# A fused adaLN transformer block on one core: the last group of block 0, the place of one k projection, and two waits of the MLP

## The chip, the cores and the metric

The kernel runs on one core of a Trainium2 chip. The metric is the device time of one execution in microseconds (us); the median of three timed runs of the kernel before is 3613.98 us (3611.85 to 3615.18). Engines are named as in the profile: PE is the matrix engine (PEld its weight loads), DVE the vector engine, ACT the scalar engine, POOL the GpSimd engine, SP the engine whose queue issues nearly all transfers.

## The reference

For eight sequences of 1024 tokens with 512 channels the reference computes one transformer block whose two normalizations are shifted and scaled by a condition:

```python
mod = silu(condition) @ Wada + bada
sh_a, sc_a, gt_a, sh_m, sc_m, gt_m = split(mod, 6, axis=1)
xm = layernorm(x, g1, be1) * (1 + sc_a) + sh_a
x = x + gt_a * attention(xm, Wqkv, Wproj, bproj)     # causal, 16 heads of 32 channels
xm = layernorm(x, g2, be2) * (1 + sc_m) + sh_m
x = x + gt_m * (gelu(xm @ W1 + b1) @ W2 + b2)        # W1: 512 x 2048, W2: 2048 x 512
```

All data are float32. In the softmax of a row, the exponentials are divided by their sum over all visible keys.

## The kernel before

**Blocks and groups.** The tokens are cut into 16 blocks of 512 (`blocks`): block n is half h = n % 2 of sequence n // 2. A block of half 0 sees 512 keys, a block of half 1 sees 1024. The 16 heads of a block are handled in four groups g of four heads. A group is cut into units of 512 columns; the triangular diagonal parts are packed, and the third triangle of an even group shares a unit with that of the odd group after it.

**Attention of one group.** `scores` makes q k^T into the one four-bank PSUM tile `st`, DVE adds the mask (L1403) and takes row maxima (L1406). `split_maxima` writes the maxima as three bf16 parts (L1425 to L1428), `maxima_rows` turns them into rows (L1444). `weights_T` then computes transposed scores minus the maxima into the same tile `st` (L1469, L1481), ACT takes the exponential into one of three SBUF slots `pT` (L1493), POOL zeroes the masked triangle (L1498). `weigh` multiplies by v into `po` (L1521). The sums of the exponentials are collected by `add_weights`: POOL adds every further unit's exponentials onto those of the group's first unit, head by head (L1594). `finish` then multiplies that one accumulated tile with a matrix of ones (L1539), which sums over the key partitions; ACT copies sums and numerators to `rec` and `top` (L1545, L1548; one buffer each), DVE inverts the sums in four reciprocals (L1554) and POOL multiplies (L1571) into the tile that held q. When `add_weights` is done with a unit, its slot goes back to `free_p`.

**The reciprocals are jobs.** `finish` does not issue the four reciprocals and the product itself; it puts them on the list `jobs`, which `run_jobs` empties one by one when, by the planner's reckoning, DVE is not behind PE.

**Linear work.** All projections (q, k, v, the MLP's up and down products) use a Strassen-like scheme of seven products instead of eight (`strassen`, `down`), all through three PSUM banks and the matmul at L201. A k, q or v projection is 7 products of 32 matmul records. Weight pieces of 256 KB come through a ring of nine buffers, filled in the order of use by `fetch` on SP whenever a piece is released. The sums of weight quarters that the scheme needs are made once: for q, k, v at the start, for W1 and W2 by the generator `preparation` (on DVE or POOL, `either`, L158 and L161), which also writes them to DRAM through SP (L687). A piece that is such a sum can be fetched only after that.

**Order of the work.** `plan[w]` lists the linear steps of window w, which is laid beside the attention of block w. Window 0 ends with `("k", 2)` and `("gates", "m")`; window 1 begins with the load of the residual of block 0, the gate rows, `("proj", 0)`, `("mt", 0)` (transposes of the normalized residual), `("q", 2)` and the up products of block 0. The steps run as one stream (`main`); parts that may run late (`tail`, `modulated`) are side threads. A step yields what it must wait for; `proj` of block n waits for `("attended", n)`, which is set when the last group's product has been issued.

**Interleaving.** The program is put in order when it is built, by a planner with costs in ns per instruction (`note`, `due`). Before each attention step, `step_aside` lets linear steps go first until they have done as much as is due by then, and further while the attention's inputs are not ready by that reckoning. What is due grows by each attention unit's need times `stream["rate"]`, which is the planned time of the window's steps over the block's need (times 0.7 in block 0). `scores` takes another way, `scores_by_heads` (L1357, L1376), when no linear step can run for the next 3000 ns: it uses the free banks for four single heads.

**Gate of the MLP.** The first up product of block 0, `("u", 0, 0)`, waits for `"prepared"`, which is set when `preparation` has made the sums of both matrices. `attend` drives all of it; the last unit of block 0's group 3 is closed (`close`, `finish`) after one more score unit, and then the remaining score units of block 1's group 0 and some of group 1 are issued.

Of the kernel before, what the change touches and what calls it, by code (L numbers as in the profile page):

```python
# [22 lines left out]
def kernel(  # L23
# [203 lines left out]
    def mlp_steps(n):  # L227
# [4 lines left out]
        + [("load_xa", 1), ("sums", "q", 0), ("k", 0), ("norm_a", 1), ("q", 0)]  # L232
        + [("sums", "v", 0), ("at", 1), ("v", 0)],
        0: [("load_xa", 2), ("preps",), ("k", 1), ("norm_a", 2), ("gates", "a"), ("q", 1)]
        + [("mod", 3), ("at", 2), ("v", 1), ("mod", 4), ("columns_m",), ("k", 2), ("gates", "m")],
    }
    late = []
    for w in range(1, NB):
        n = w - 1
        m = mlp_steps(n)  # L240
        even = blocks[n][1] == 0
        rows_a = [("rows", blocks[n][0], "a")] if even else []
        rows_m = [("rows", blocks[n][0], "m")] if even else []
        own = m[:1] + ([("load_xa", w + 2)] if w + 2 < NB else []) + m[1:3]
        own += [("norm_a", w + 2)] if w + 2 < NB else []
        if w == NB - 1:
            steps = late[:1] + [("load_xr", n)] + rows_a + [("proj", n), ("mt", n)] + late[1:]
            steps += [("v", w)] + rows_m + own + m[3:6]
            late = m[6:]
        else:  # L250

            steps = late + [("v", w), ("load_xr", n)] + rows_a + [("proj", n), ("k", w + 1)]
            if w == 1:
                steps = [("load_xr", n)] + rows_a + [("proj", n)]
            steps += [("mt", n), ("q", w + 1)] + rows_m + own
            at = [("at", w + 2)] if w + 2 < NB else []
            if blocks[w][1] == 0:

                steps += m[3:5]
                late = m[5:6] + at + m[6:]  # L260
            else:
                steps += m[3:6] + at
                late = m[6:]
        plan[w] = steps
# [440 lines left out]
    def preparation():  # L705


        todo = [(w, i) for w in (W1, W2) for i in range(NQ)]
        loaded = []

        def load(w, i):
            stage = act.tile([P, NC, TB], F32, tag="hT", name=f"prep_{LABEL[id(w)]}_{i}", bufs=NQ)
            got = {}
            for j, kf in enumerate(RAW):
                a = next(a for a in ("A11", "A12", "A21", "A22") if FULL[a] == kf)
                got[a] = stage[:, j, :]
                nc.sync.dma_start(got[a].rearrange("p (k n) -> p k n", n=HB), quarter(w, i, *kf))
            loaded.append((w, i, got, now["PE"] + 12000))

        load(*todo.pop(0))  # L720
        while loaded:
            if todo:
                load(*todo.pop(0))
            w, i, got, ready = loaded.pop(0)
            for out, a, b, op, name in IN_PLACE:
                yield ready
                keys = [("prep", w is W2, i, a), ("prep", w is W2, i, b)]
                either(got[out], got[a], got[b], op, keys, [("prep", w is W2, i, out)])
                keep(w, i, name, got[out])
# [209 lines left out]
    def up(step):  # L939
        _, n, q = step  # L940

        def gelu():
            for i in range(NC):
                f = q * NC + i
                nc.scalar.activation(  # L945
                    hT[:, i, :], hT[:, i, :], AF.Gelu, bias=cols[:, O_B1 + f : O_B1 + f + 1]
                )
                k = q // 2 + 1
                note_act(590, "gelu", [("h", n, q)], [(n, f"B{k}1"), (n, f"B{k}2"), ("g", n, q)])

        def finished():
            if q == NQ - 1:
                written["m used", n] = 0.0
            excursion(gelu, [("h", n, q)], first=True)

        if (n, q) == (0, 0):
            yield ["prepared"], []
        written["g", n, q] = NEVER
        hT = act.tile([P, NC, TB], F32, tag="hT", name=f"hT_{n}_{q}", bufs=NQ)
        hTs[n, q] = hT  # L960

        yield from strassen(
            step,
            f"m{n}",
            lambda f, t: hT[:, half(f, 2), half(t, HB)],
            ("h", n, q),
            False,
            finished,
        )
# [18 lines left out]
    def down(n, part):  # L988
# [79 lines left out]

        got = partials
        if part == 0:  # L1070
            yield [("g", n, 0), ("g", n, 1)], []
            for i in range(NTT):
                add_to(residual[n][:, i, :], gate_rows["gbm"], [("row", "gbm")], [("xr", n, i)])
            combine(nc.vector, "B12", "B12", "B11")
# [47 lines left out]
    def perform(step):  # L1122
# [28 lines left out]
        elif kind == "at":  # L1151
            n = step[1]
            guards = [("m used", n - 3)] if n > 2 else [("v done", 0)] if n == 2 else []
            start(modulated(f"a{n}", *columns_of["a"], blocks[n][0], guards))
        elif kind == "beside":
            start(perform(step[1]))
        elif kind == "sums":
            sum_weights(step[1:])
        elif kind == "mt":
            n = step[1]  # L1160
            guards = [("v done", n + 1)]
            start(modulated(f"m{n}", *columns_of["m"], blocks[n][0], guards))
        elif kind == "k":
            yield [("free for k", step[1])], []
            yield from project_T(step, kTs, kvp, "kT", lambda: None)
        elif kind == "q":
            yield from project_T(step, qTs, act, "qT", lambda: projected.add(step[1]))
        elif kind == "v":
            yield from project_v(step)
        elif kind == "preps":  # L1170
            prepared[0] = [preparation(), 0.0]
            written["prepared"] = NEVER
        elif kind == "rows":
            gate_broadcasts(*step[1:])
        elif kind == "proj":
            yield from project_out(step[1])
        elif kind == "u":
            yield from up(step)
        elif kind == "d":
            yield from down(*step[1:])  # L1180
# [272 lines left out]
            m_rows[n, g] = row  # L1453

    free_p = list(range(3))
    outs, totals = {}, {}

    def weights_T(n, g, parts):
# [72 lines left out]
    def finish(n, g):  # L1531

        run_jobs(True)
        acc, slot = totals.pop((n, g))
        step_aside([("acc", n, g)], [BANK])
        bank = lin_bank()
        for j in range(HPG):
            r = slice(j * hd, (j + 1) * hd)
            nc.tensor.matmul(banks[bank][r, :], ones[:, :hd], acc[:, j, :], start=True, stop=True)  # L1539
        note_pe(2 * COLUMN * TB, "columns", [("acc", n, g), ("p", slot)], [("l", bank)])  # L1540
        free_p.append(slot)
        top = tmp.tile([P, TB], F32, tag="top", name=f"top_{n}_{g}", bufs=1)
        rec = tmp.tile([P, TB], F32, tag="rec", name=f"rec_{n}_{g}", bufs=1)
        kr = "rec"
# [12 lines left out]
        if (n, g) == groups[-1]:  # L1557
# [4 lines left out]
                note("DVE", 200, [kr, "top"], [("att", n, i)])  # L1562
            return

        def quotient():
            invert(3)
            if n == NB - 1 and g == NC - 2:
# [13 lines left out]

    def add_weights(n, g, parts, pT, slot):

        acc, first = totals[n, g]
        for _, c0, w, _ in parts:
            for j in range(HPG):
# [65 lines left out]
    def close(n, g, parts, pT, slot, last):  # L1652
# [3 lines left out]
        weigh(n, g, own, pT, slot, last)  # L1656
        if other:
            shared[n, g + 1] = other, pT, slot
        elif parts[0][0] > 0:
            free_p.append(slot)  # L1660
        if parts[0][0] == 0:
            totals[n, g] = (pT, slot)
            if (n, g) in shared:
                more, pT, slot = shared.pop((n, g))
                weigh(n, g, more, pT, slot, False)
                add_weights(n, g, more, pT, slot)
                free_p.append(slot)
        if last:
            finish(n, g)

# [97 lines left out]
```

## Time and profile before

| what | value |
|---|---|
| median of three timed runs | 3613.98 us |
| the profiled execution: first to last instruction | 3610.1 us |
| PE busy | 3537.6 us, 98% |
| DVE, ACT, POOL busy | 58%, 37%, 56% |
| mean granted PE clock | 0.995 |
| transfers on SP's queue | 422.56 MB, 38.8% of the 16 DMA engines |

The page gives no time of the profiled execution other than its span; the timed runs are 1.7 to 5.1 us above it, which holds what lies around the first and the last instruction. In the timeline a row is a run of equal instructions: start, length, engine, line, operation, output <- inputs, shapes, count, and in brackets the idle time before it with what ended it. A float32 matmul of the program appears as two records, and four matmuls of 32 columns each run beside one another, so "x8" is one matmul for each of the four heads or column groups. A window row gives the busy time of each engine in a stretch, then the granted PE clock, the busy share of the DMA engines and their rate.

### The profile page before, as it was taken

What the parts mean: (1) busy time and instruction counts of PE and PEld (TensorE: products, weight loads), DVE (VectorE), ACT (ScalarE), POOL (GpSimd) and SP (SyncE); (2) the same over time, 40 slices, a digit from 0 to 9 for tenths busy, and PEclk for the clock granted to TensorE, in tenths of its full rate; (3) what the DMA queues carried; (4) which work ended last, traced back from release to release, by engine and by line L of the source; (5) the groups of instructions that cost most, each with busy time, mean ns of one, the idle gap of its engine ahead of it and who ended that gap; (6) DMA issues with size and microseconds to landing.
All of it is one profiled execution on the core that took longest, in us unless ns stands there. A gap on an engine that the chain in (4) does not pass through costs nothing.

```text
span 3610.1 us, 121129 instructions
## 1 busy us (share of the span) xinstructions
PE 3537.6 (98%) x54821; PEld 1777.0 (49%) x54821; DVE 2078.8 (58%) x2316; ACT 1325.9 (37%) x1388; POOL 2038.3 (56%) x2187
## 2 busy tenths in 40 slices
PE   8999999999999999999999999999999999999999
PEld 5434445445554455544555455454554545545445
DVE  6765675563755547465464655746557455564663
ACT  2335334252433523335243351424524244232421
POOL 3666746665456753666536665456654566544660
PEclk9989999999999999999999999999999999999999
DMA  6633333434343343433434334343343433435334
GB/s 202 220 117 104 109 104 110 127 98 128 112 118 110 104 133 113 133 92 98 133 109 148 91 93 132 105 141 101 99 128 105 139 101 101 124 92 155 90 111 138
DMA packets 307894, 430.35 MB, mean 119 GB/s; under 512 B 25900, under 2 KB 176236, under 8 KB 307380
## 3 DMA queue, kind: packets, MB, share of 16 engines
q1 hardware_dynamic: 307264, 422.56, 38.8%
q8 instruction: 432, 7.08, 0.8%
q14 instruction: 82, 0.67, 0.1%
q10 hardware_dynamic: 116, 0.03, 0.0%
HBM read 394.12 MB, written 28.38 MB: 117 GB/s over the span
## 4 chain that ended last, share of the span: by engine, by line
PE 90%; DVE 4%; POOL 2%; ACT 2%; issue 1%; DMA 0%; SPq 0%; ACTq 0%; DVEq 0%; POOLq 0%
PE bank L201 62%; PE st L1469 8%; PE sc L1389 8%; PE po L1521 7%; DVE mx L1406 2%; PE st L1481 2%; PE bank L641 2%; PE bank L1539 2%; POOL pT L1594 1%; POOL xr L161 1%; ACT pT L1493 1%; DVE hT L1003 0%; PE bank L1444 0%; DVE xr L158 0%; ACT hT L945 0%
## 5 line engine op out<-in xcount | busy, mean ns | idle before, releaser
L1594 POOL TENSOR_TENSOR pT<-pT,pT 128x384 f32<-128x384 f32 (+2 forms) x1266 | 1195.6, 981 | 400.4 <-PE po L1521 211.0
L1493 ACT ACTIVATE pT<-st 128x2048 f32<-128x2048 f32 x288 | 541.0, 1878 | 858.2 <-PE st L1481 826.5
L201 PE MATMUL bank<-w,hT 128*32 128x256 f32 x14336 | 805.6, 381 | 1.0 <-ACT rec L1545 0.9
L1406 DVE TENSOR_REDUCE mx<-sc 128x4 f32<-128x2048 f32 (+3 forms) x380 | 658.5, 1754 | 147.7 <-PE sc L1389 140.6
L201 PEld LDWEIGHTS bank<-w,hT 128*32 128x32 f32 x14336 | 455.2, 110 | 338.4 <-issue 42.7
L201 PE MATMUL bank<-xm_m,w 128*32 128x256 f32 x8192 | 498.3, 381 | 3.1 <-ACT xm_m L651 3.0
L201 PE MATMUL bank<-t_m,w 128*32 128x256 f32 x6144 | 392.2, 381 | 0.4 <-DVE t_m L660 0.4
L1498 POOL TENSOR_SCALAR_AFFINE_SELECT pT<-pT 128x512 f32<-128x512 f32 x256 | 162.1, 651 | 400.4 <-ACT pT L1493 400.4
L201 PEld LDWEIGHTS bank<-xm_m,w 128*32 128x32 f32 x8192 | 254.9, 110 | 229.9 <-issue 62.5
L1389 PE MATMUL sc<-kT,qT 32*128 32x512 f32 (+3 forms) x3040 | 331.6, 524 | 7.6 <-DVE mx L1406 7.0
L1469 PE MATMUL st<-qT,kT 32*128 32x512 f32 (+3 forms) x3072 | 330.9, 523 | 6.7 <-DVE mx L1406 5.0
L1403 DVE TENSOR_TENSOR sc<-sc,mask 128x1024 f32<-128x1024 f32 (+1 forms) x159 | 161.5, 1016 | 278.9 <-PE sc L1389 238.9
L1521 PE MATMUL po<-pT,v 128*32 128x512 f32 (+3 forms) x3072 | 305.8, 493 | 10.2 <-POOL pT L1498 10.2
L201 PEld LDWEIGHTS bank<-t_m,w 128*32 128x32 f32 x6144 | 187.1, 110 | 197.2 <-issue 81.7
L201 PE MATMUL bank<-xm_a,w 128*32 128x256 f32 x3968 | 239.8, 380 | 0.0
L201 PE MATMUL bank<-w,qT 128*32 128x512 f32 x2048 | 237.8, 595 | 0.0
L1554 DVE RECIPROCAL rec<-rec 128x128 f32<-128x128 f32 x256 | 226.0, 919 | 6.0 <-ACT rec L1545 6.0
L1389 PEld LDWEIGHTS sc<-kT,qT 32*128 32x128 f32 x3040 | 130.8, 184 | 175.7 <-ACT pT L1493 81.3
L1469 PEld LDWEIGHTS st<-qT,kT 32*128 32x128 f32 x3072 | 130.1, 184 | 164.4 <-issue 71.6
L1493 ACT ACT_TABLE_LOAD x88 | 112.9, 1283 | 205.8 <-PE st L1481 205.3
L201 PE MATMUL bank<-t_a,w 128*32 128x256 f32 x2944 | 188.5, 380 | 0.0
L193 DVE TENSOR_TENSOR hT<-bank,u_u 128x512 f32<-128x512 f32 x192 | 128.4, 683 | 97.0 <-PE bank L201 96.2
(207 smaller groups left out, 3521.3 us busy)
## 6 DMA issues: line engine op xcount, KB each, us to landing
w<-in_L_cond_W_dram SPq DMA_DIRECT2D x384, 256.0 KB
w<-kept_up_S SPq DMA_DIRECT2D x256, 256.0 KB
w<-kept_down_S SPq DMA_DIRECT2D x256, 256.0 KB
w<-kept_qkv_S SPq DMA_DIRECT2D x180, 256.0 KB
w<-in_L_cond_Wqkv_dram SPq DMA_DIRECT2D x147, 256.0 KB
hat<-in_x_dram SPq DMA_DIRECT2D x64, 256.0 KB
w<-in_L_cond_Wproj_dram SPq DMA_DIRECT2D x64, 256.0 KB
xr<-in_x_dram SPq DMA_DIRECT2D x64, 256.0 KB
```

What stands on the lines that cost most here:

```text
L193: nc.vector.tensor_tensor(out, src, other, op)
L201: nc.tensor.matmul(ps[r, :], lhsT[:, r], rhs, start=start, stop=stop, skip_group_check=True)
L641: nc.tensor.transpose(banks[bank][:, ts(t, P)], got[t][:, ts(c, P)], ident)
L1389: nc.tensor.matmul(sc[:, j, c0 : c0 + w], qTs[n][r, gg, ts(qt, P)], keys_of(n, kh)[r, gg, :w], start=True, stop=True, skip_group_check=True,)
L1403: nc.vector.tensor_tensor(place, place, shape_of.to_broadcast(place.shape), ALU.add)
L1406: nc.vector.tensor_reduce(maxima[n, gg][:, kh, qt, :], sc[:, :, c0 : c0 + w], axis=AX.X, op=ALU.max)
L1469: nc.tensor.matmul(st[:, j, c0 : c0 + w], kT[r, gg, ts(k % NTT, P)], qT[r, gg, TB - w :], start=(c0 == 0), stop=False, skip_group_check=True,)
L1493: nc.scalar.activation(pT[:, :, :used], st[:, :, :used], AF.Exp, scale=scale)
L1498: nc.gpsimd.affine_select(diagonal, diagonal, pattern=[[0, HPG], [1, P]], compare_op=ALU.is_ge, fill=0.0, base=0, channel_multiplier=-1,)
L1521: nc.tensor.matmul(po[r, TB - w :], v[:, k % NTT, g * P + j * hd : g * P + (j + 1) * hd], pT[:, j, c0 : c0 + w], start=(k == 0), stop=last ...
L1554: nc.vector.reciprocal(some, some)
L1594: nc.gpsimd.tensor_tensor(into, into, pT[:, j, c0 : c0 + w], ALU.add)
```

## The change

The plan moves `("k", 2)` from the end of window 0 to window 1, between the gate rows and `("proj", 0)`; `("gates", "m")` therefore follows `("columns_m",)` directly. In block 0's group 3 (`first_end`), `add_weights` no longer adds on POOL but keeps the units in `unadded`; their slots are held until `finish`, which sums all terms by ones matmuls into one bank, and then issues the four reciprocals and the product at once, the product on DVE. The wait for the weight sums is split: `"prepared up"` is set when the sums of W1 are done and is what the first up product waits for; every block's first down part now also waits for `"prepared"`.

```diff
         0: [("load_xa", 2), ("preps",), ("k", 1), ("norm_a", 2), ("gates", "a"), ("q", 1)]
-        + [("mod", 3), ("at", 2), ("v", 1), ("mod", 4), ("columns_m",), ("k", 2), ("gates", "m")],
+        + [("mod", 3), ("at", 2), ("v", 1), ("mod", 4), ("columns_m",), ("gates", "m")],
...
             if w == 1:
-                steps = [("load_xr", n)] + rows_a + [("proj", n)]
+                steps = [("load_xr", n)] + rows_a + [("k", w + 1), ("proj", n)]
...
             w, i, got, ready = loaded.pop(0)
+            if (w is W2, i) == (True, 0):
+                written["prepared up"] = 0.0
...
         if (n, q) == (0, 0):
-            yield ["prepared"], []
+            yield ["prepared up"], []
...
         if part == 0:
-            yield [("g", n, 0), ("g", n, 1)], []
+            yield [("g", n, 0), ("g", n, 1), "prepared"], []
...
-            written["prepared"] = NEVER
+            written["prepared up"] = written["prepared"] = NEVER
...
+    first_end, unadded = (0, NC - 1), []
...
-        step_aside([("acc", n, g)], [BANK])
+        more = unadded if (n, g) == first_end else []
+        step_aside([("acc", n, g), *(("p", slot) for *_, slot in more)], [BANK])
         bank = lin_bank()
-        for j in range(HPG):
-            r = slice(j * hd, (j + 1) * hd)
-            nc.tensor.matmul(banks[bank][r, :], ones[:, :hd], acc[:, j, :], start=True, stop=True)
-        note_pe(2 * COLUMN * TB, "columns", [("acc", n, g), ("p", slot)], [("l", bank)])
-        free_p.append(slot)
+        terms = [(0, TB, acc, slot)] + [(c0, w, pT, slot) for parts, pT, slot in more for _, c0, w, _ in parts]
+        for i, (c0, w, term, held) in enumerate(terms):
+            for j in range(HPG):
+                r = slice(j * hd, (j + 1) * hd)
+                nc.tensor.matmul(
+                    banks[bank][r, TB - w :], ones[:, :hd], term[:, j, c0 : c0 + w],
+                    start=i == 0, stop=i == len(terms) - 1, skip_group_check=True,
+                )
+            note_pe(2 * COLUMN * w, "columns", [("acc", n, g), ("p", held)], [("l", bank)])
+        free_p.extend([slot, *(held for *_, held in more)])
...
+        if (n, g) == first_end:
+            for i in range(NTT):
+                invert(i)
+            nc.vector.tensor_tensor(qTs[n][:, g, :], top, rec, ALU.mult)
+            note("DVE", 700, [kr, "top"], [("att", n)], port=True)
+            written["attended", n] = 0.0
+            return
...
     def add_weights(n, g, parts, pT, slot):
 
+        if (n, g) == first_end:
+            unadded.append((parts, pT, slot))
+            return
...
-        elif parts[0][0] > 0:
+        elif parts[0][0] > 0 and (n, g) != first_end:
             free_p.append(slot)
...
-                free_p.append(slot)
+                if (n, g) != first_end:
+                    free_p.append(slot)
```

## The prediction

> **What bounds the kernel now.** I read the page first, then the list of what PE waited for, then windows around the longest of these waits, then each engine's timeline there.
>
> ```profile
> span 3610.1 us, 121129 instructions
> PE 3537.6 (98%) x54821; PEld 1777.0 (49%) x54821; DVE 2078.8 (58%) x2316; ACT 1325.9 (37%) x1388; POOL 2038.3 (56%) x2187
> ```
>
> PE is the bound nearly everywhere, so a change can only win where PE stands or is slow. The waits list names one group above all, the scores by heads that wait for DVE. The windows show the place and a second price, the granted clock (PEclk):
>
> ```profile
> core 0: us, PE busy (x) PEld busy (x) DVE busy (x) ACT busy (x) POOL busy (x), PEclk, DMA share, GB/s
> 166.40:174.00 7.60, 7.57 (x56) 3.08 (x51) 5.85 (x6) 1.07 (x2) 5.62 (x6) 1.00 0.89 277
> 174.00:178.60 4.60, 0.14 (x4) 0.14 (x8) 4.53 (x7) 0.00 (x0) 4.37 (x4) 1.00 1.05 391
> 178.60:185.50 6.90, 4.48 (x26) 2.58 (x26) 6.76 (x13) 0.00 (x0) 0.23 (x1) 0.75 0.75 241
> 185.50:199.20 13.70, 10.46 (x50) 3.55 (x54) 12.47 (x15) 1.02 (x2) 6.92 (x9) 0.50 0.79 285
> 248.20:250.40 2.20, 0.16 (x5) 0.09 (x1) 1.74 (x3) 2.19 (x6) 0.00 (x0) 0.99 0.00 0
> 250.40:257.20 6.80, 6.55 (x32) 3.82 (x32) 3.74 (x3) 4.78 (x7) 0.00 (x0) 0.50 0.00 0
> ```
>
> PE work lost = length minus busy time times clock. 174.0 to 178.6: 4.60 - 0.14 = 4.5; to 185.5: 6.90 - 4.48 x 0.75 = 3.5; to 199.2: 13.70 - 10.46 x 0.50 = 8.5. Together **16.5 us**. The last two rows, another stall, lose 2.0 + 3.5 = 5.5. What PE lacked in the first stall:
>
> ```profile
> 157.30 9.23 POOL L1594 TENSOR_TENSOR pT<-pT,pT 128x256 f32<-128x256 f32 x12
> 195.80 1.26 POOL L1571 TENSOR_TENSOR qT<-top,rec 128x512 f32<-128x512 f32 x1 [3.61 <-DVE rec L1554]
> ```
> ```profile
> 173.43 0.93 DVE L1554 RECIPROCAL rec<-rec 128x128 f32<-128x128 f32 x1
> 181.71 0.94 DVE L1554 RECIPROCAL rec<-rec 128x128 f32<-128x128 f32 x1
> 187.96 0.94 DVE L1554 RECIPROCAL rec<-rec 128x128 f32<-128x128 f32 x1
> 194.72 0.94 DVE L1554 RECIPROCAL rec<-rec 128x128 f32<-128x128 f32 x1
> ```
> ```profile
> 178.46 0.81 PE L1357 MATMUL bank<-kT,qT 32*128 32x384 f32 x1 [4.49 <-DVE mx L1376]
> 198.66 3.01 PE L201 MATMUL bank<-w,qT 128*32 128x512 f32 x24
> ```
>
> The ones matmul of block 0's group 3 waits for twelve POOL additions (to 166.5). Its four reciprocals then lie on DVE one by one between score reductions, over 21 us, and only then POOL makes the product. Projection 0 (w,qT) starts at 198.66. In front of it the linear stream is empty, and score units, which DVE takes 2.3 to 3.6 us each for, are all PE has.
>
> **The change part by part.**
>
> *Sums on PE.* Twelve POOL additions (9.23 us) go. In their place come ones matmuls of 384, 128 and 256 columns. In `po` rows of this shape 384 + 128 take 0.86 us in the chain and 256 take 0.46, so **+1.3 us** on PE. The last `po` of the group ends at 159.2, so the sums can end at 159.2 + 0.86 + 1.3 = 161.4 instead of 168. Three `pT` slots stay held until then, which is no later than before (166.8), so the next exponentials wait for nothing new.
>
> *Weighed against the skill.* The Trainium skill, "Perfetto Trace Analysis", Identifying the Most-Contended Engine, says to improve the engine with the highest occupancy first. Read so, this part is wrong way round: PE has 98%, POOL 56%, and the sum would be +1.3 us and nothing gained. The window rows of 174 to 199 decide for me: there PE is not the contended engine.
>
> *Reciprocals at once.* `rec` and `top` have one buffer, so ACT's copy waits for group 2's product. That stood behind the additions (166.49); without them it follows group 2's last reciprocal (161.8) and ends at 163.1. Then: copy 0.58, four reciprocals 4 x 0.92 = 3.7, product. The product moves from POOL (1.28) to DVE; its one row there is 1.64 us, other DVE products of two SBUF tiles of this size 0.68 to 1.7, so 0.7 to 1.7. A score reduction of 2.29 may lie in front. The result stands at 163.1 + 0.6 + 3.7 + 0.7 to 1.7 + 0 to 2.3 = 168.1 to 171.4, against 197.1. Queued behind these 4.4 to 5.4 us on DVE are one reduction and one bank's copy; PE has three banks and other work, so I cost that wait at nothing, and at up to 2.3 us if the banks are all full.
>
> *k 2 as cover.* 7 x 32 records at 1.72 us per 32: 12.0 us, moved, not added. Gates m (16 records, 3.6 us) now come first. Between 148 and 159.2 the stream took 72 records, 3.9 us; so 15.6 - 3.9 = 11.7 us of it remain, plus the sums 2.2 and seven score units of 1.07 each (7.5): 21.4 us of PE work for the 9 to 12 us until the result stands. The cover is enough, after it come projection 0 (13.7 us at full clock) and q 2 (12.0). So the 16.5 us should go wholly; for a bound below, DVE may hold up part of it (18.66 of 20 us busy in 180 to 200), and I set 10 to 16.5.
>
> *Transfers of the moved steps.* On SP, gates m's two bias rows, four weight pieces and two kept rows go ahead of k 2's seven pieces, and the residual's four loads (0.43 us each) and two gate rows (0.33) go out some 20 us earlier. The ring runs nine pieces ahead; PE's waits for such pieces were 3.3 us in all, at start-up, and one of 2.1 at 109.7. I take 0, bound 0 to 2. All share SP with the W2 sums' writes, which in the profile occupy the queue from 190.9 for 18.0 us waiting for sums; behind them stand q 2's last two pieces and the first up pieces (issued 219.6 to 221.3, when projection 0 released them).
>
> *The MLP gate.* W1's last sum ended at 166.2, W2's at 208.5; the first up matmul ran at 256.6. Both gates were open. Even 15 us earlier both are: 0. The new wait of the first down part (339.5) is as open; behind it is nothing.
>
> *What is late next.* First, block 0's normalization: q 2 was its only cover and is still; it lost 5.5 us. It will come when DVE also has W2's sums (six took 9.1 us), so I add 2 (0 to 5). Second, projection 1:
>
> ```profile
> 429.53 1.28 POOL L1571 TENSOR_TENSOR qT<-top,rec 128x512 f32<-128x512 f32 x1
> ```
> ```profile
> 440.68 1.89 PE L201 MATMUL bank<-w,qT 128*32 128x512 f32 x16
> ```
>
> Its input stood 9.9 us before it was used. If the linear stream runs 13.7 us (projection 0) ahead of block 1's attention, whose single score buffer sets its pace, 13.7 - 9.9 = 3.8 us are missing; attention fills part, and a slow clock follows. I take 3 (0 to 8.7, twice the rest of the lead and a slow clock). The later projections, the last excepted, had 41 to 75 us of slack by the same two rows of the timeline, so nothing follows from there.
>
> *The clock after a stall.* Here gaps of 2.04 and 2.47 us were followed by 6.8 and 3.4 us at half clock, and of four gaps of 2.06 us two by 3.4 us. The Trainium skill, "TensorE: Matmul & The Clock Gate", HAM oscillation, puts the danger at idle gaps of over about 3.4 us. By that rule the missing time at projection 1 would cost itself alone, some 1.5 us, and the sum would be 1.5 better. I go by the rows.
>
> **Sum:** -16.5 + 1.3 + 2 + 3 = -10.2. The profiled execution's 3610.1 becomes 3599.9; the runs' median is 3.9 above it, so **3604 us**.
>
> **Rivals.**
> 1. *All recovered.* Block 1's attention starts earlier too, projection 1 waits for nothing, the normalization is no later: -16.5 + 1.3 = -15.2, 3599; with the normalization's 5.5 covered as well 3593. For it: attention no longer waits behind reciprocals. Against: DVE's 18.66 of 20.
> 2. *The stall moves.* Block 1 starts no earlier, the whole lead of 15.2 meets the slack of 9.9: 5.3 idle and 3.4 for the clock, 8.7, and the normalization 5 more: 15.2 - 13.7 = 1.5, 3612. The single score buffer speaks for it, pacing against it.
> 3. *It does not do what it says.* Weight pieces of q 2 queue on SP behind the 18.0 us of W2 writes and PE stands there instead: 16.5 - 1.3 - 18 to 0, 3602 to 3617, middle 3610. Against: five of q 2's seven pieces were fetched by 174.
> 4. *Slower: the pacing of later blocks.* Moving k 2 out of a window weighted 0.7 into one weighted 1 raises what is due by 0.3 of a k projection, 3.6 us by the planner's own units, for all later windows. In the profile some block pairs have one gap of 2.06 us (POOL, L1498). If the new offset gives each of six later pairs one more, with 3.4 us at half clock, that is 3.8 each, 22.6: -10.2 + 22.6 = +12, 3626. It decides from five pairs on. Nothing in the trace excludes it.
>
> **How the numbers follow.** Forecast 0.54 (its own range 3599 to 3606.5), rival 1 0.14, rival 2 0.13, rival 3 0.07, rival 4 0.12. 0.2% (7.2 us) is about what a measurement can tell from no change. Faster (under 3606.8): 0.54 + 0.14 = 0.68. Same: rivals 2 and 3, 0.20. Slower: 0.12. The range runs from rival 1's end, 3593, to 3616; only rival 4 and the last microsecond of rival 3 lie beyond.
>
> **What would show it.** Right: no L1357 group at all (no scores by heads); projection 0's first matmul at 168 to 182; four reciprocals of block 0's group 3 back to back; no L1594 of 384 columns at 157 to 166; clock 1.00 through 160 to 200; PE waits at `xh_m` near 225 and possibly at `w,qT` near 420. Wrong: PE waiting for DMA on w in 180 to 210 (rival 3), a gap of several us in front of projection 1 (rival 2), or more waits of `po` for L1498 past 500 us (rival 4). I am also wrong if DVE, not the empty stream, carried the stall: then PE idles on bank waits in 160 to 200 though projection 0 has begun.

## The result, and the profile after

| kernel | median of 5 runs | ratio to before (95%) | profiled execution | its span | clock |
|---|---|---|---|---|---|
| before | 3613.98 us | 1 | | 3610.1 us | 0.995 |
| after | 3598.27 us (3596.36 to 3606.11) | 0.9957 (0.9945 to 0.9969) | 3596.36 us | 3594.6 us | 0.998 |

The change makes the kernel 0.43% faster. The forecast was 3604, with 3593 to 3616 around it. In the two profiled executions the span, from the first to the last instruction, is 15.5 us shorter. In every run that has both numbers the time is 1.6 to 1.8 us above the run's own span; so of the 3.9 us that the forecast added to the span of before, about 2.1 say only that this profiled execution was a little faster than the median.

The page of after, to be held against the same lines of before:

```profile
span 3594.6 us, 121150 instructions
PE 3529.1 (98%) x54845; PEld 1774.2 (49%) x54845; DVE 2073.7 (58%) x2296; ACT 1328.0 (37%) x1395; POOL 2045.4 (57%) x2176
```

PE shows 24 records more (the new ones matmuls) and yet 8.5 us less busy time: time at half clock counts as busy, and there is less of it. The mean clock has gone from 0.995 to 0.998.

Block 0's end, in the timelines of after (start, length, engine, line; the lines of the changed file lie 2 to 20 further down than in before):

```profile
159.61 2.34 PE L1545 MATMUL bank<-pT,ones 128*32 128x512 f32 x32
166.21 3.66 PE L201 MATMUL bank<-xm_a,w 128*32 128x256 f32 x64 [0.90 <-ACT p_k L188]
172.67 1.14 PE L1391 MATMUL sc<-kT,qT 32*128 32x512 f32 x8 [1.08 <-DVE mx L1408]
173.74 1.07 PE L201 MATMUL bank<-w,qT 128*32 128x512 f32 x8
```
```profile
165.21 3.39 DVE L1563 RECIPROCAL rec<-rec 128x128 f32<-128x128 f32 x4 [2.01 <-ACT rec L1554]
168.70 1.72 DVE L1577 TENSOR_TENSOR qT<-top,rec 128x512 f32<-128x512 f32 x1
170.34 2.28 DVE L1408 TENSOR_REDUCE mx<-sc 128x4 f32<-128x2048 f32 x1
```

The sums (L1545, 32 records) end at 161.9. The four reciprocals lie back to back, and the result of group 3 stands at 170.4 (before: 197.1). Projection 0 (`w,qT`) starts at 173.74 instead of 198.66. The two gaps in brackets, 0.90 and 1.08, are all that is left of the 16.5 us.

Two sets of windows of after (columns: length, busy time of each engine with its instructions, granted clock, DMA share, GB/s): block 0's end up to the first up product, and a stretch near the end of block 1's attention.

```profile
core 0: us, PE busy (x) PEld busy (x) DVE busy (x) ACT busy (x) POOL busy (x), PEclk, DMA share, GB/s
165.00:173.80 8.80, 6.82 (x116) 3.39 (x112) 8.38 (x8) 1.74 (x4) 4.64 (x4) 1.00 0.93 323
173.80:196.00 22.20, 22.20 (x246) 8.00 (x248) 18.21 (x18) 0.00 (x0) 17.20 (x17) 1.00 0.73 255
196.00:222.20 26.20, 26.20 (x340) 10.98 (x335) 14.72 (x21) 16.50 (x16) 20.83 (x17) 1.00 0.57 192
399.40:415.70 16.30, 9.96 (x88) 3.29 (x80) 3.69 (x8) 4.69 (x4) 13.88 (x17) 0.79 0.09 34
```

From 173.8 to 222.2 PE is never idle and at full clock: the stall of 174 to 199 is gone, and so is the one of 248 to 257, in block 0's normalization. The last row is a new stall. In 16.3 us PE is busy 9.96 us at 0.79 of the clock, so 16.3 - 9.96 x 0.79 = 8.4 us of PE work are lost by this row. Counted record by record, as idle time plus half of the time that PE was busy at half clock, they are 7.9: 6.3 idle and 1.6 by the clock. Its gaps in the timeline of after:

```profile
403.09 0.69 PE L1359 MATMUL bank<-kT,qT 32*128 32x512 f32 x1 [1.10 <-DVE mx L1378]
406.76 1.07 PE L1524 MATMUL po<-pT,v 128*32 128x384 f32 x16 [1.48 <-POOL pT L1501]
411.58 3.15 PE L1545 MATMUL bank<-pT,ones 128*32 128x512 f32 x8 [3.75 <-POOL pT L1614]
415.74 1.93 PE L201 MATMUL bank<-w,xm_a 128*32 128x256 f32 x32
429.50 1.89 PE L201 MATMUL bank<-w,qT 128*32 128x512 f32 x16
```

No matmul of the linear stream (L201) runs between 397.4 and 415.74. The one that then starts is v 2's first (`w,xm_a`), and the L1545 ahead of it is the last ones matmul of block 1. Projection 1 follows only at 429.50.

**Where the 15.5 us came from.** Projection 2's last matmul ends at 677.8 before and 670.3 after: 7.5 us of the gain lie ahead of it, 8.0 behind it. The windows from there to the end, of before and then of after:

```profile
677.80:3610.10 2932.30, 2897.15 (x45022) 1456.61 (x45020) 1653.40 (x1829) 1088.48 (x1141) 1647.63 (x1747) 1.00 0.39 115
```
```profile
670.30:3594.60 2924.30, 2893.06 (x45020) 1460.50 (x45020) 1647.52 (x1818) 1089.99 (x1147) 1656.82 (x1749) 1.00 0.38 115
```

The work is the same (45,022 and 45,020 records). PE is idle 2932.3 - 2897.2 = 35.2 us before and 31.2 after, 3.9 less; the records at half clock lose 5.1 us of work before and 1.6 after, 3.5 less; 0.6 is left. Nothing of the change stands in this code. What differs is the order, by the planner's pace.

In the first part, lost PE work, counted record by record, falls by 11.8 us: -15.1 at block 0's end (17.0 to 2.0; the prediction's windows, with one mean clock for each, gave 16.5), -5.5 in its normalization, +7.9 at 402 to 415, and +0.9 over all other places. Of these, a wait for a later block's normalized input (2.47 us at 395 before) appears at 606 instead. The new ones matmuls add 1.3. The rest, 11.8 - 1.3 - 7.5 = 3.0 us more of busy time in after, is not explained.

### The profile page after: what moved, and what is told of

It reads as the page before. It is cut to its first block, busy times and chain, and to the rows that moved or that the text cites. A ratio compares the mean times of both kernels' runs of the same rounds, so it can differ in the third digit from the quotient of the medians.

```text
span 3594.6 us, 121150 instructions
## 1 busy us (share of the span) xinstructions
PE 3529.1 (98%) x54845; PEld 1774.2 (49%) x54845; DVE 2073.7 (58%) x2296; ACT 1328.0 (37%) x1395; POOL 2045.4 (57%) x2176
## 4 chain that ended last, share of the span: by engine, by line
PE 89%; DVE 5%; POOL 3%; ACT 2%; issue 1%; DMA 1%; SPq 0%; ACTq 0%; DVEq 0%; POOLq 0%
PE bank L201 62%; PE sc L1391 8%; PE st L1472 8%; PE po L1524 7%; DVE mx L1408 2%; PE st L1484 2%; PE bank L1545 2%; PE bank L641 1%; POOL pT L1614 1%; ACT pT L1496 1%; DMA w<-in_L_cond_Wada_dram 1%; POOL xr L161 1%; DVE xr L158 0%; PE bank L1446 0%; DVE hT L1005 0%
## 5 line engine op out<-in xcount | busy, mean ns | idle before, releaser
L1614 POOL TENSOR_TENSOR pT<-pT,pT 128x256 f32<-128x256 f32 (+3 forms) x1254 | 1188.1, 983 | 430.6 <-PE po L1524 241.4
L201 PE MATMUL bank<-w,hT 128*32 128x256 f32 x14336 | 807.5, 380 | 1.2 <-ACT rec L1554 0.9
L201 PEld LDWEIGHTS bank<-w,hT 128*32 128x32 f32 x14336 | 454.8, 110 | 346.3 <-issue 54.2
L201 PE MATMUL bank<-xm_m,w 128*32 128x256 f32 x8192 | 496.0, 380 | 3.2 <-ACT xm_m L651 3.0
L201 PE MATMUL bank<-t_m,w 128*32 128x256 f32 x6144 | 388.7, 381 | 0.5 <-DVE t_m L660 0.5
L201 PEld LDWEIGHTS bank<-xm_m,w 128*32 128x32 f32 x8192 | 255.4, 110 | 225.9 <-issue 58.6
L201 PEld LDWEIGHTS bank<-t_m,w 128*32 128x32 f32 x6144 | 188.3, 110 | 192.0 <-issue 75.5
L201 PE MATMUL bank<-xm_a,w 128*32 128x256 f32 x3968 | 240.3, 380 | 0.9 <-ACT p_k L188 0.9
L201 PE MATMUL bank<-w,qT 128*32 128x512 f32 x2048 | 237.4, 594 | 0.0
L201 PE MATMUL bank<-t_a,w 128*32 128x256 f32 x2944 | 188.3, 380 | 0.0
L1427 POOL CAST mcols<-mx 128x16 bf16<-128x16 f32 x61 | 15.6, 256 | 289.9 <-DVE mx L1422 157.0
```

The lines of the kernel that those rows point to most:

```text
L201: nc.tensor.matmul(ps[r, :], lhsT[:, r], rhs, start=start, stop=stop, skip_group_check=True)
L1614: nc.gpsimd.tensor_tensor(into, into, pT[:, j, c0 : c0 + w], ALU.add)
```

## The experiments

All are medians; the ratio is to the kernel before on the same chip (3614.2 to 3614.9 us there). "Rest" is the time from projection 2's end to the last instruction in the profiled execution.

| kernel | median us | ratio (95%) | projection 2 ends | rest |
|---|---|---|---|---|
| e1: before, k 2 moved | 3609.29 | 0.9986 (0.9977 to 0.9996) | 678.2 | 2926.7 |
| e2: after, k 2 not moved | 3620.80 | 1.0021 (1.0010 to 1.0032) | 690.1 | 2934.6 |
| e3: after, reciprocals as jobs | 3603.29 | 0.9968 (0.9956 to 0.9980) | 674.7 | 2925.6 |
| e4: after, sums on POOL | 3607.40 | 0.9981 (0.9972 to 0.9990) | 677.5 | 2926.2 |
| e5: after, old pace | 3601.47 | 0.9963 (0.9950 to 0.9975) | 667.2 | 2930.5 |
| e6: before, new pace | 3608.60 | 0.9982 (0.9973 to 0.9991) | 684.0 | 2927.7 |
| e7: after, a score unit first | 3602.72 | 0.9970 (0.9960 to 0.9981) | 676.4 | 2924.6 |
| e8: e7, and block 1's reciprocals at once | 3603.35 | 0.9972 (0.9960 to 0.9983) | 674.5 | 2926.5 |
| e9: after again | 3597.61 | 0.9952 (0.9940 to 0.9965) | 674.0 | 2926.1 |
| e10: after, three v buffers | 3598.75 | 0.9952 (0.9939 to 0.9966) | 671.0 | 2926.8 |
| e11: after, k 3 ahead of v 2 | 3595.42 | 0.9946 (0.9932 to 0.9959) | 665.2 | 2927.1 |

### The parts of the change: e1 to e4

**e1** moves k 2 alone, in the kernel before.

```diff
-        + [("mod", 3), ("at", 2), ("v", 1), ("mod", 4), ("columns_m",), ("k", 2), ("gates", "m")],
+        + [("mod", 3), ("at", 2), ("v", 1), ("mod", 4), ("columns_m",), ("gates", "m")],
...
-                steps = [("load_xr", n)] + rows_a + [("proj", n)]
+                steps = [("load_xr", n)] + rows_a + [("k", w + 1), ("proj", n)]
```

> The kernel before with the k projection moved and nothing else. Theory A (the early result does it): projection 0 still waits for a result that stands at about 185 to 197 us, and k 2 and gates m lie ahead of projection 0 in both orders, so the PE work available before it is the same 15.6 us; scores by heads and 10 us or more of lost PE work remain, total 3607 to 3615 us. Rival B (k 2 is the cover): most of the stall goes without the other edits, total 3598 to 3603.

Measured 3609.29, 0.9986. The stall stays: 15.0 us of PE work are lost in 160 to 220, where before loses 17.0. What PE waited for in 160 to 200 us of e1 (engine, line, releaser: us in total, times, longest):

```profile
PE bank L1357 <- DVE mx L1376: 8.0, 3, 3.8
```

Group 3's result stands at 196.5, and projection 2 ends at 678.2, 0.4 later than in before. The whole gain, about 5 us, lies behind that: rest 2926.7 against 2932.3. So the move alone does little for block 0's end and changes the order of later blocks.

**e2** takes back the move alone. Projection 0 must then also wait for the deferred end (`tail`) of k 2, a wait that before does not have; so e2 prices the missing move and this wait together.

```diff
-        + [("mod", 3), ("at", 2), ("v", 1), ("mod", 4), ("columns_m",), ("gates", "m")],
+        + [("mod", 3), ("at", 2), ("v", 1), ("mod", 4), ("columns_m",), ("k", 2), ("gates", "m")],
...
-                steps = [("load_xr", n)] + rows_a + [("k", w + 1), ("proj", n)]
+                steps = [("load_xr", n)] + rows_a + [("proj", n)]
...
-        yield [("attended", n)], []
+        yield [("attended", n)] + ([tail_key[0]] if n == 0 else []), []
```

> The changed kernel with k 2 back in window 0, ahead of gates m (projection 0 also waits for k 2's last two products, whose pieces must leave the ring first). Theory A: nothing lost at projection 0, which starts at 168 to 182 us; total within 4 us of the changed kernel, 3595 to 3603. Rival B: without the cover the stream is empty from about 165 us, projection 0 waits, total 3606 or more.

Measured 3620.80, 1.0021 (1.0010 to 1.0032): slower than before. The result of group 3 stands at 172.2 without the move too, and there is no wait for it. But projection 0 stops on a weight piece. Timelines of PE and of SP's queue in e2:

```profile
179.03 1.90 PE L201 MATMUL bank<-w,qT 128*32 128x512 f32 x16
190.47 5.05 PE L201 MATMUL bank<-w,qT 128*32 128x512 f32 x32 [6.76 <-DMA w<-in_L_cond_Wproj_dram]
```
```profile
183.32 0.38 SPq L339 DMA_DIRECT2D w<-in_L_cond_Wproj_dram  x1
```

The piece was issued at 183.3, once k 2's last pieces had left the ring and the loads of the gate rows and the residual had gone ahead of it on SP. More follows up to block 1's end, at 437.7: lost PE work is 23.8 us between 206.9 and 476.4. The rest, 2934.6, is that of the old pace. So my heading "k 2 as cover" was loose: k 2 and gates m, 15.6 us, lie ahead of projection 0 in both orders. By this trace the move matters through what stands at the end of the ring, and through the pace. The total lies in the range of rival B, but its reason, an empty stream, is not what PE waited for. That e2 is worse than before as a whole I did not expect; which of its later gaps follow from the one at 183.7 no run isolates.

**e3** keeps the new sums, but leaves reciprocals and product to the list of jobs.

```diff
-        if (n, g) == first_end:
-            for i in range(NTT):
-                invert(i)
-            nc.vector.tensor_tensor(qTs[n][:, g, :], top, rec, ALU.mult)
-            note("DVE", 700, [kr, "top"], [("att", n)], port=True)
-            written["attended", n] = 0.0
-            return
```

> The changed kernel with the four reciprocals and the product as jobs again (product on POOL), sums still by ones matmuls. Theory A: the sums end at 162 us, but the reciprocals lie between score reductions, so the result stands at 176 to 190 us instead of 170.4 and part of the stall is back: 3600 to 3609. Rival C (the POOL additions alone were the delay): no stall, within 3 us of the changed kernel.

Measured 3603.29, inside the expected interval. DVE's timeline in e3 shows that they spread again:

```profile
182.06 0.93 DVE L1563 RECIPROCAL rec<-rec 128x128 f32<-128x128 f32 x1
186.85 0.93 DVE L1563 RECIPROCAL rec<-rec 128x128 f32<-128x128 f32 x1
191.58 1.75 DVE L1563 RECIPROCAL rec<-rec 128x128 f32<-128x128 f32 x2
```

The result stands at 195.0, later than I expected and nearly where it stood before. PE's waits in 160 to 200 are 6.5 us and half clock lasts from 186.0 to 196.3. So the additions alone were not the delay, as rival C had it. Against after (3597.6 and 3598.3), reciprocals at once are worth some 5 us in the medians; the intervals overlap (0.9956 to 0.9980 and 0.9945 to 0.9969), so this size is rough.

**e4** keeps the reciprocals at once, with the sums on POOL as before.

```diff
     def add_weights(n, g, parts, pT, slot):
 
-        if (n, g) == first_end:
-            unadded.append((parts, pT, slot))
-            return
...
-        elif parts[0][0] > 0 and (n, g) != first_end:
+        elif parts[0][0] > 0:
             free_p.append(slot)
...
-                if (n, g) != first_end:
-                    free_p.append(slot)
+                free_p.append(slot)
```

> The changed kernel with the twelve POOL additions back and one ones matmul, reciprocals still at once. Theory A: the sums end at 168 us, the result stands at about 175, the stream runs dry at about 172 to 178, so 0 to 4 us are lost and 1.3 us of PE work saved: 3597 to 3602. Rival C (the additions were the delay): half of the gain or more goes, 3605 or more.

Measured 3607.40, above the 3597 to 3602 expected of my theory and in the range of rival C. The place itself went as my theory had it: the sums end at 169.4, the result stands at 175.0, projection 0 starts at 173.0, and PE loses 1.5 us there (2.0 in after). The loss came later. PE's timeline in e4:

```profile
173.00 2.76 PE L201 MATMUL bank<-w,qT 128*32 128x512 f32 x24
220.07 2.01 PE L1472 MATMUL st<-qT,kT 32*128 32x512 f32 x8 [4.35 <-DVE mx L1408]
405.15 2.09 PE L1472 MATMUL st<-qT,kT 32*128 32x512 f32 x8 [5.25 <-DVE mcols L1427]
```

The first gap lies in block 0's normalization (the reciprocal of its deviation ends at 216.4; in after at 209.5), the second at block 1's end. So the delay (sums 7.4 us later than in after, result 4.6) cost nothing where it arose; against after, the kernel is 9 to 10 us slower all the same, by gaps in the next 250 us. Keeping the sums on PE is worth that, though they are 24 more records for the engine that is busy 98%. What goes wrong first between 175 and 216 no run isolates. The trace shows that the planner gives five of W2's 16 sums back to DVE in e4, where after has all 16 on POOL.

### The pace: e5 and e6

What is due in a window grows with `rate`. Moving k 2 takes its cost out of window 0's rate (weighted 0.7) and puts it into window 1's. e5 gives after the old rates, e6 gives before the new ones (the same lines with the signs of `costs["k"]` exchanged). No step moves in either.

```diff
-            stream["rate"] = planned_time(n) / mine * (0.7 if n == 0 else 1.0)
+            moved = {0: costs["k"], 1: -costs["k"]}.get(n, 0)
+            stream["rate"] = (planned_time(n) + moved) / mine * (0.7 if n == 0 else 1.0)
```

> The changed kernel with the weights of windows 0 and 1 counted as if k 2 still lay in window 0 (what is due later is 3.6 us less, as before); nothing else moves. Theory D (the pace gave part of the gain): the span up to the end of projection 2 stays at 670 to 673 us, and from there to the end it is 2930 to 2935 us as before instead of 2924, total 3602 to 3609. Rival E (the later blocks differ by chance, not by the pace): 3595 to 3601.

> The kernel before with only the pace of the change (window 0 counted without k 2, window 1 with it), the order of steps and the end of group 3 as before. Theory D: the stall of 174 to 199 us stays, the later blocks win 5 to 8 us, total 3605 to 3610. Rival E: no change, 3611 to 3616.

e5: 3601.47, half a microsecond under what was expected of the pace (and projection 2 ends at 667.2, ahead of the 670 to 673 expected). e6: 3608.60, inside. Over all runs read, the rest of the kernel takes 2924.3 to 2927.7 with the new pace (after, e1, e3, e4, e6 to e11) and 2930.5 to 2934.6 with the old one (before, e2, e5), whatever was done at block 0's end. PE's idle time in it is 30.8 to 31.4 us in the ten executions with the new pace and 34.8 to 35.2 in the three with the old one. That is shown. How much it is in a median is less sharp: e1 and e6 gain 5 to 6 us, after loses 3 to 4 when it gives the pace up, and the intervals of after and e5 overlap. The kind of gap is seen where PE waited for POOL's triangles in that stretch, before and then after:

```profile
PE po L1521 <- POOL pT L1498: 10.2, 6, 2.1
```
```profile
PE po L1524 <- POOL pT L1501: 7.1, 4, 2.1
```

Two gaps of six are gone, and the half clock that followed two of the old ones.

### The new stall at 402 to 415: e7 to e11

In after, after the sums, PE waits 0.90 and 1.08 us around the reciprocals, with no score unit in between. **e7** issues one score unit of block 1 ahead of the reciprocals, to see whether block 1's end then comes earlier.

```diff
         if (n, g) == first_end:
+            ns = score_need(*units[unit_at[0]])
+            next_scores()
+            pace(ns)
             for i in range(NTT):
                 invert(i)
```

> The changed kernel with one score unit of block 1 issued ahead of the four reciprocals, so that its reduction takes the 2.0 us in which DVE waits for ACT's copy. Theory F (the new stall at 402 to 415 us comes from v 2 waiting for block 1's end, and block 1 starts late because its scores wait behind the reciprocals): the gap of 10.8 us between two score units goes, block 1's last ones matmul comes 3 to 8 us earlier than 413.7, the stall there shrinks, total 3590 to 3597. Rival G (block 1's start does not set its end): the last ones matmul stays within 2 us, total 3595 to 3602.

Measured 3602.72. PE's timeline of e7 has the score units close together:

```profile
163.88 1.14 PE L1391 MATMUL sc<-kT,qT 32*128 32x512 f32 x8
167.43 1.14 PE L1391 MATMUL sc<-kT,qT 32*128 32x512 f32 x8
418.38 2.28 PE L1545 MATMUL bank<-pT,ones 128*32 128x512 f32 x8 [1.02 <-POOL pT L1617]
```

But the last ones matmul of block 1 (the third row) runs to 420.7, not earlier than the 414.7 of after, and the stall there is larger (gaps of 5.25, 1.17, 1.10 and 1.02). Theory F falls: the second score unit of block 1 comes 5 us earlier than in after, and block 1's end comes 6 us later.

**e8** adds to e7 that block 1's last group, too, does its reciprocals at once, in case the stall waits for block 1's result.

```diff
-        if (n, g) == first_end:
-            ns = score_need(*units[unit_at[0]])
-            next_scores()
-            pace(ns)
+        if g == NC - 1 and n < 2:
+            if n == 0:
+                ns = score_need(*units[unit_at[0]])
+                next_scores()
+                pace(ns)
             for i in range(NTT):
                 invert(i)
```

> As the run with one score unit ahead, and the four reciprocals and the product of block 1's last group at once on DVE too. Theory F: projection 1 then waits for v 2's end alone; 0 to 3 us better than that run. Rival: the result was not waited for, no difference (within 2 us) or 1 to 2 us worse for the DVE time.

Measured 3603.35, the same as e7. Block 1's result stands at 423.8, and projection 1 uses it at 433.7, 9.9 us later. Nothing waits for it; the same gaps stay.

**e9** is after once more, on the chip of the next two.

> The changed kernel itself on the chip of this call, as the measure for the two others: 3596 to 3601 us.

Measured 3597.61. Its profiled execution lies 5 us behind the first one of after already at projection 0's end: a gap of 2.08 us at 112.4, in the start-up, was followed by 6.8 us at half clock; a gap of 2.26 us at nearly the same place in the first execution was followed by none. Differences of a few microseconds between two profiled executions are no evidence by themselves; the medians are.

**e10** gives v a third buffer, so that v 2 need not wait until block 1 has read v 0's. To make room, the gate bias rows aren't loaded: the gate rows are added in their place, and two small tiles are cut down. So e10 leaves the biases out of the output and their loads out of the time.

```diff
...
-        for name in (f"g{kind}", f"gb{kind}"):
-            row = rowp.tile([P, D], F32, tag=f"row{name}", name=f"row_{name}_{b}")
-            nc.sync.dma_start(row, kept_rows[name][b : b + 1, :].to_broadcast([P, D]))
-            gate_rows[name] = row
+        name = f"g{kind}"
+        row = rowp.tile([P, D], F32, tag=f"row{name}", name=f"row_{name}_{b}")
+        nc.sync.dma_start(row, kept_rows[name][b : b + 1, :].to_broadcast([P, D]))
+        gate_rows[name] = gate_rows[f"gb{kind}"] = row
...
-        v = kvp.tile([P, NTT, D], F32, tag="v", name=f"v_{n}", bufs=2)
+        v = kvp.tile([P, NTT, D], F32, tag="v", name=f"v_{n}", bufs=3)
...
-        if n > 1:
+        if n > 2:
             written["free for v", n] = NEVER
```

> The changed kernel with a third buffer for v and no wait of v 2 for block 1's end. To make room, the bias rows of the gates are left out: the gate rows themselves are added in their place, with their loads. Theory H (the stream runs dry at v 2, which waits for a buffer that block 1 reads to its end): v 2 starts before 405 instead of 415.7, PE's waits in 400 to 415 go; projection 1 then waits for block 1's result, which stands at about 421 to 427 us, so 2 to 6 us of the 8 come back there; 3590 to 3598. Rival I (attention itself stands in 402 to 415, whatever linear work is free): the waits of po for L1501 and of the ones matmul for POOL stay, total unchanged within 2 us.

Measured 3598.75. PE's timeline of e10:

```profile
401.34 1.48 PE L201 MATMUL bank<-w,xm_a 128*32 128x256 f32 x24
421.65 1.47 PE L1472 MATMUL st<-qT,kT 32*128 32x384 f32 x16 [2.48 <-DVE mx L1408]
433.50 2.09 PE L1472 MATMUL st<-qT,kT 32*128 32x512 f32 x8 [3.30 <-DVE mx L1408]
436.80 4.91 PE L201 MATMUL bank<-w,qT 128*32 128x512 f32 x32
```

v 2 starts at 401.34, and the gaps of 402 to 415 are gone. So the wait was for v's buffer. But the time doesn't fall: now PE stands in front of projection 1 (436.80), with gaps of 2.48 and 3.30 us and half clock after both. That is the place that the prediction had named, one step later than where after stands.

**e11** puts work there instead: k 3 ahead of v 2.

```diff
+            if w == 2:
+                steps = late + [("k", w + 1), ("v", w), ("load_xr", n)] + rows_a + [("proj", n)]
...
-            written["free for k", n + 2 if n % 2 else n + 1] = 0.0
+            if n != 1:
+                written["free for k", n + 2 if n % 2 else n + 1] = 0.0
...
                 pT, slot = weights_T(n, g, parts)
+                if (n, g, k) == (1, NC - 1, NTT - 1):
+                    written["free for k", n + 2] = 0.0
```

> The changed kernel with k 3 ahead of v 2 in window 2, free as soon as block 1's last unit of the first half's keys is through. Theory H: 12 us of linear work fill 402 to 414, the stall of about 8 us there goes, projection 1 waits for nothing; block 1's normalization has lost k 3 as cover (0 to 4 us back): 3588 to 3596. Rival I: unchanged within 2 us, or slower through the lost cover.

Measured 3595.42, the fastest, though its interval (0.9932 to 0.9959) overlaps that of after on the same chip (0.9940 to 0.9965). Lost PE work from 196 to 454 us is down to 2.3. But block 1's normalization has now lost k 3 as its cover. What PE waited for in 395 to 500 us of e11:

```profile
PE bank L643 <- ACT xh_m L582: 2.5, 4, 1.8
PE st L1474 <- DVE rstd_m L567: 2.0, 1, 2.0
```

With 478.2 to 488.4 at half clock, PE loses 8.4 us from 454 to 500, where after loses 0.4. That is as much as was gained ahead of it (10.3 to 2.3). After e10 this is the second time that a removed wait comes back one step further on.

## Why the prediction was right

The time was right (3604 for 3598, the sign at 0.68), and in part by luck: it is the sum of one right main term, two right small ones, one with the wrong sign, one too small, and one that was left at nothing.

- **The stall, -16.5 (bounds 10 to 16.5): -15.1 record by record, -14.5 by the prediction's windows.** Its reason held. Result forecast at 168.1 to 171.4, measured 170.4; projection 0 forecast at 168 to 182, measured 173.74; no scores by heads there; clock 1.00. The sign "no L1357 group at all" went too far: of the 32 records of scores by heads, 8 come back (L1359) at the new stall of 400.8 to 404.2. Of the two halves it is the reciprocals at once that remove this stall (e4 has them alone, and the result at 175.0; e3 has the sums alone, and it at 195.0); the sums pay later. The prediction weighed the sums against the Trainium skill ("Perfetto Trace Analysis", Identifying the Most-Contended Engine), which has the engine with the highest occupancy improved first, and took PE's 98% for that occupancy. The same passage sets TensorE apart: there it wants the work done against the peak, and the busy share of the weight loads, in place of the matmuls' busy share. The weight loads (PEld) are busy 49% here, less than POOL's 56% and DVE's 58%, so by that share the page does not speak against the move (the work against the peak no run here gives), and e4 against after shows that the sums on PE gain some 9 us. No mean over the span told which engine had room in these 25 us; the windows did.
- **Sums on PE, +1.3: right.** 32 records in 2.34 us, where 8 took 1.04.
- **k 2 as cover.** The work is ahead of projection 0 with or without the move, as e2 shows; my count of it (21.4 us for 9 to 12) was right, calling it the move's doing was not. "Transfers: 0" held for the order of the change. Rival 3, weight pieces queued on SP, did not happen in after: PE's waits in 160 to 230 name no DMA. e2 shows a wait of that kind, 6.76 us, but for a piece of projection 0 and not behind W2's writes. (The gap of 2.1 us at 109.7 in before, which the prediction counts as a wait for a piece, is put down by the profile to no transfer: its row names "issue".)
- **The MLP gate, 0: right.** W2's last sum ends at about 206, the first up matmul runs at 223.0. With the old single gate put back, the order of instructions on every engine is the same, so there is nothing to measure.
- **Block 0's normalization, +2 (0 to 5): wrong sign, -5.5.** I reckoned that W2's sums would delay it. In after the four statistics run together from 201.6, 5.6 us after projection 0's end at 196.0, and its transposes lie between q 2's matmuls from 213.9. In before one ran at 223.4 and the other three at 234.6 to 236.9, 12.5 us after projection 0's end at 222.1. The premise that DVE would also have W2's sums did not come true: in before DVE took six of the 16 and three of the additions to the residual, in after it took none, and POOL took all. That fits the earlier statistics, but no run isolates it; e4 and its gap of 4.35 us at 215.7 show only that it doesn't follow from an earlier projection 0 alone.
- **Projection 1, +3 (0 to 8.7): right kind, wrong step, too small.** The stream does run ahead of block 1's attention and block 1's score buffer does set the pace. But ahead of projection 1 comes v 2, which needs the buffer that block 1 reads to its end. I had counted the slack of projection 1's input and not that of v 2's buffer. It cost 7.9 us, not 3, as half clock came on top (407.9 to 414.7). e10 shows both: with a free buffer for v a loss of the same kind arises in front of projection 1.
- **Later blocks, priced at nothing: -8.0 in the profiles, 3 to 6 in the medians of e1, e5 and e6.** This is rival 4's mechanism with the other sign. I had worked out the offset (3.6 us by the planner's units) and seen the gaps of 2.06 us that it could shift, and then let it only add gaps. It could take them away as well, and did.

The local sum was forecast at -10.2. The measured terms make -15.1 + 1.3 - 5.5 + 7.9 + 0.9 = -10.5, so the errors at the normalization and at v 2 cancel; that is luck. With the 3.0 us that are not explained it is -7.5. The other 8.0 of the 15.5 lie behind projection 2, which the prediction had at nothing; the pace alone is worth 3 to 6 of them in the medians.

**The clock.** I reckoned with half clock after gaps of 2.0 to 2.5 us. After shows it from a shorter one too, in its windows where PE waited for ACT and a normalized input (`xm_a`):

```profile
606.00:609.30 3.30, 1.58 (x12) 1.00 (x10) 3.23 (x4) 3.23 (x4) 3.30 (x3) 0.99 0.06 21
609.30:612.70 3.40, 3.25 (x46) 1.67 (x48) 3.30 (x2) 1.57 (x3) 3.40 (x2) 0.50 0.02 5
```

The gap in the first row is 1.70 us; 3.4 us at 0.50 follow. A threshold of about 3.4 us of idling, as the Trainium skill gives it ("TensorE: Matmul & The Clock Gate", HAM oscillation), would price such gaps at themselves alone; the measurement decides for more.

The clock records of all 13 traces show what the length of a gap leaves out. Every stretch at one clock, full or half, that ends within an execution is a whole number of slices of 3.41 us long (half clock: 3.4, 6.8, 10.2, 13.7 or 23.9 us), so the clock changes on a fixed grid. Laid on this grid, all 55 full-clock slices in which PE was busy at most 40% were followed by half clock, 22 of the 87 with 40 to 60% were, and none of the 13,381 with more. The prediction's gaps of 2.06 us in before fit: those at 1691.8 and 3019.7 lie whole in one slice (40% busy) and were followed by half clock; those at 2136 and 2578 are cut by an edge (58% and 45% busy in the emptier slice) and were not. What decides between 40 and 60% no run shows.

## What to carry to other kernels

When a late result makes an engine stand that is busy nearly all the time, price the stretch and not the mean: 25 us at block 0's end lost some 17, and adding work to the "full" engine there shortened the kernel. Then follow the recovered time to the next thing that is shared between blocks, by every resource that a step waits for (a buffer as well as an input): it came back at v 2's buffer, with that freed at projection 1, and with that filled at the next normalization. Where a planner lays out the work, moving a step also changes its pace for all that follows; give that a term with both signs, and measure it by changing the rate alone.

## What the runs showed of the hardware

- The granted clock changed only at the edges of slices of 3.41 us, and what a gap cost went by how much of one slice PE stood, not by the gap's length alone. A gap of 1.70 us was followed by 3.4 us at half clock (606 to 613 in after; the slice 50% busy), while gaps of 2.06 us at 2136 and 2578 in before were not followed by any. In the start-up of after, a gap of 2.26 us at 110, cut by an edge (59% busy in the emptier slice), was followed by none in its first profiled execution, and in its second one (e9) a gap of 2.08 us at 112 (51%) by 6.8 us.
- The product of two 128 x 512 tiles in SBUF took DVE 1.72 us (L1577) while POOL was at work for most of it; the same product of block 1's last group in e8 took 0.69 at 423.1, where POOL stood idle from 418.4 to 427.4. A DVE operation of the same size and type that reads a bank took 0.68 at block 0's end.
- Four reciprocals back to back took 3.39 us; alone one took 0.93, so 4 x 0.93 - 3.39 = 0.33 us are saved by the row.
